# Moving stores behind their copies, and a strided bias load, in a fused scan, attention and experts kernel

## Chip, cores and metric

The kernel runs on one core of one Trainium2 chip, written in Bass with the Tile layer under a manual schedule. The metric is device time in microseconds (us), the median of three runs. All data are 32-bit floats.

## What is computed

Four images of 384 channels and 32x32 positions go through two layers. The reference, cut to what matters:

```python
# layer 0: four-direction selective scan, B=4, D=384, L=1024, N=16 states
x = x + _L0_conv_ref(_gn(x), ...)
#   per direction k: dt = softplus(W_dt (W_x x)); Bs, Cs = rows of W_x x
    def step(h, inp):
        dtt, ut, bt, ct = inp
        dA = jnp.exp(dtt[..., None] * A)
        h = h * dA + (dtt * ut)[..., None] * bt[:, :, None, :]
        y = jnp.einsum('bkdn,bkn->bkd', h, ct)
        return (h, y)
#   the four directions are summed, normalised over channels, gelu
# layer 1: attention over 1024 tokens (one head of 384, causal), then 4 experts, top 2
t = _to_tokens(x)
t = t + _L1_attn_ref(_ln_t(t), Wq, Wk, Wv)
t = t + _L1_ffn_ref(_ln_t(t), gate_w, gate_b, w1, b1, w2, b2)
#   ffn: h = gelu(x w1 + b1); y = h w2 + b2; out = sum of gate * y over the chosen two
x = _from_tokens(t, x)
```

## The kernel before, in words

The scan sets the clock of the whole program. It is cut into 768 units: 4 images (b), 3 blocks of 128 channels (m), 4 directions (k), 4 groups of 4 states (q), 4 groups of 32 channels (j). Each unit is a tile of 128 partitions (32 channels by 4 states) by 1024 positions. the main loop (from L2090 on) runs a counter `t`, the tick, and emits one unit's work in each: `decay` on ScalarE (ACT) makes `da` = exp(dt * a); `front` (L705) on VectorE (DVE) makes `v` = du * B; `middle` (L711) on DVE is the scan itself, h = h * da + v; `back` (L728) on GpSimd (POOL) multiplies h by C; `row` (L753) on TensorE (PE), every fourth tick, sums over the states into `y` in PSUM. For the first image, part of the `v` tiles are made on PE and ACT instead (`feed` and `turned`, L1017).

Beside the scan, `preparation(b)` makes the inputs of the next image: group norm, the projections, softplus, and in `project_dt` the product du = dt * u (L576). It stores dt and du in DRAM (L578, L579). `fetch` loads them back, repeated over the states: dt five ticks ahead of its use (L666, four buffers), du three ticks ahead (L666), and the B and C rows (`bc`, L677, two buffers, one pair of loads in four ticks) three ticks ahead. These loads, and nearly all others, are issued by SyncE (SP), which takes its instructions strictly in the order in which they were emitted.

Layer 1 of image b runs beside the scan of image b+1. `attention` makes the scores, the softmax and the values; `rows` (from L1236) takes each block of 128 tokens out of PSUM with an ACT copy into `yb` (L1240) and stores it to `t2_d` at once (L1242). `experts` runs 11 blocks of 256 tokens, each through two weight matrices, six weight tiles for each (L1627); `out_` copies a block's result to the tile `yt` on ACT (L1793), stores it to `ys_d` at once (L1795), and gives the tile's slot back. Later `combine` gathers these rows (L1832), reads `t2_d` again, and writes the output. The last image has no scan beside it: its attention and experts (`alone` in the code) form the tail of the kernel.

The work in a tick is ordered by hand. A generator yields `"wait", n` to go on n ticks later. `defer(n, f)` runs `f` at the start of tick t + n; with `inner` as third argument, in the middle of it. The tiles of layer 1, of the preparation and of the weights share eight `slots`: a generator that finds none free waits for the next tick, and a slot that is given may be taken a tick later. All this is decided when the program is built; on the chip only semaphores hold the engines to it.

`later` runs once, from tick 8 on: it loads small constants, one DMA a tick (L333), among them the bias b2 of the experts in three loads, each turned from expert-last to expert-first by its access pattern (4x128 single values); then it sums `d_skip` on DVE (L336), waits 40 ticks, zeroes a tile on POOL (L339), and stores it over the tables `xs_d` and `ys_d` in eight DMAs of 1.5 MB, six ticks apart (L343). In `within`, a flag is computed on DVE that chooses a cheaper softplus; one tick later (L514) POOL and ACT are told to load it (L515).

Of the kernel before, what the change touches and what calls it, by code (L numbers as in the profile page):

```python
# [17 lines left out]
P = 128  # L18
B = 4
C = 384  # L20
M = C // P
# [33 lines left out]
NBLK = 2 * L // BT + E - 1  # L55
# [3 lines left out]
def hybrid_kernel(  # L59
# [22 lines left out]
    nc = tc.nc  # L82
# [41 lines left out]
    def defer(ticks, f, where=due):  # L124
        where.setdefault(clock[0] + ticks, []).append(f)

    class Shared:
# [6 lines left out]
        def ready(self, n=1):  # L134
            return len(self.free) >= n and self.free[n - 1][0] <= clock[0]
# [69 lines left out]
    t2_d = [dram.tile([L, C], F32, tag=f"t2_{b}", name=f"t2d_{b}") for b in range(B)]  # L205
# [113 lines left out]
    b2s = const.tile([E, C], F32, tag="b2s", name="b2s")  # L319
# [6 lines left out]
    def later():  # L326
        yield "wait", 8
        for t, src in (
            (dsk, d_skip), (lnw, ln_w), (lnb, ln_b),
            (gw, gate_w.rearrange("(c p) e -> p c e", p=P)), (gb, gate_b.partition_broadcast(P)),  # L330
            *((b2s[:, m * P : (m + 1) * P], b2[:, :, m].rearrange("p e -> e p")) for m in range(M)),
        ):
            nc.sync.dma_start(t, src)  # L333
            yield "wait", 1
        yield "wait", 2
        nc.vector.tensor_reduce(dsum, dsk, AX.X, ALU.add)  # L336
        yield "wait", 40
        zero = yield from slots.take("zero", P, C)
        nc.gpsimd.memset(zero, 0.0)  # L339
        yield "wait", 2  # L340
        for t in (*xs_d, *ys_d):
            for o in range(0, E * CAP, 8 * P):
                nc.sync.dma_start(  # L343
                    t[o : o + 8 * P, :].rearrange("(r p) d -> p r d", p=P),
                    zero.unsqueeze(1).to_broadcast([P, 8, C]),
                )
                yield "wait", 6
        slots.give("zero")

# [148 lines left out]
    def within(b, xd):  # L500

        top = sm.tile([P, 1], F32, tag="top", name=f"top_{b}")
        nc.vector.tensor_reduce(top, xd, AX.X, ALU.max, apply_absolute_value=True)
        nc.vector.tensor_mul(top, top, steep)
        yield "wait", 1
        ps = yield from banks.take(f"top_{b}")
        nc.tensor.matmul(ps[:1, :K], top, mine_k, start=True, stop=True)
        yield "wait", 1
        most = sm.tile([1, 1], F32, tag="most", name=f"most_{b}")
        nc.vector.tensor_reduce(most, ps[:1, :K], AX.X, ALU.max)  # L510
        banks.give(f"top_{b}")
        fit = sm.tile([1, 1], I32, tag="fit", name=f"fit_{b}")
        nc.vector.tensor_tensor(fit, most, room, ALU.is_le)
        yield "wait", 1  # L514
        fits[b] = nc.values_load(  # L515
            fit, engines=[mybir.EngineType.Pool, mybir.EngineType.Activation],
            min_val=0, max_val=1,
        )
# [584 lines left out]
    def attention(b, yb, fx0):  # L1103

        alone = b == B - 1
# [17 lines left out]
        for h in range(NH):  # L1123
            for m in range(M):
                s = bass.ts(h, 512)
# [85 lines left out]
        def group_rows(q0, n):  # L1211

            if q0 + n > 4 and b not in routes:
                routes[b] = Route(b)
            return [
                fx0[:, q, :] if q < 4 else routes[b].rows[:, q - 4, :] for q in range(q0, q0 + n)
            ]
# [3 lines left out]
        def values(i):  # L1221
            name = f"po_{b}_{i}"
            po = yield from banks.take(name)
            s = bass.ts(i, P)
            for m in range(M):
                nc.tensor.matmul(
                    po[:, m * P : (m + 1) * P], yb[:, m, s], ident, start=(m == 0), stop=False
                )
            for j in range(i + 1):
                nc.tensor.matmul(  # L1230
                    po[:, :C], pts[i][:, j, :], vt[:, j, :], start=False, stop=(j == i)
                )
            yield "pe", 1.2 + 0.65 * (i + 1)
            slots.give(f"pt_{b}_{i}")

            def rows():  # L1236
                stat = sm.tile([P, 6], F32, tag="stat", name=f"stat_{b}_{i}")
                nc.vector.bn_stats(stat, po[:, :C])
                nc.vector.bn_aggr(moments[:, i, :], stat)
                nc.scalar.copy(yb[:, :, s], po[:, :C].rearrange("p (m t) -> p m t", m=M))  # L1240
                banks.give(name)
                nc.sync.dma_start(  # L1242
                    t2_d[b][s, :].rearrange("p (m t) -> p m t", m=M), yb[:, :, s]
                )
                for h, (q0, n) in enumerate(GROUPS):
                    if i == q0 + n - 1:
                        defer(1, lambda h=h, q0=q0, n=n: side.append(
                            ready(b, h, yb, group_rows(q0, n), moments)
                        ))

            defer(1, rows, inner)
# [334 lines left out]
    def experts(b, route):  # L1586

        alone = b == B - 1
# [42 lines left out]
        def need(key):  # L1631

            n = chunks.index(key)
            while fetched[0] <= n:
                while not slots.ready():
                    yield "wait", 1
                weights()
            while fetched[0] < min(n + 4, len(chunks)) and slots.ready(1 + slots.kept):
                weights()

        def rows_of(t, j):
            return t.rearrange("(k i p) d -> k p i d", p=P, i=BT // P)[bass.ds(block[j], 1)].rearrange(
                "o p i d -> p (o i) d"
            )
# [41 lines left out]
        def by_rows(j, run, fill):  # L1686

            if not alone:
                run(BT)
                return  # L1690
            with tc.If(filled[j] > P) as whole:
                run(BT)
            with whole.Else():
                fill(P)
                with tc.If(filled[j] > 0) as some:
                    run(P)
                with some.Else():
                    fill(0)
# [57 lines left out]
        def second_(j, gone):  # L1756
            pss = {}
            for c0 in range(0, 6, STEP):
                for c in range(c0, c0 + STEP):
                    yield from need(("2", j, c))  # L1760
                if c0 == 0:
                    for i in range(2):
                        pss[i] = yield from banks.take(f"py_{b}_{j}_{i}")
                    while clock[0] < gone:

                        yield "wait", 1

                def run(n):
                    for c in range(c0, c0 + STEP):
                        for f in range(2):  # L1770
                            for i in range(n // P):
                                nc.tensor.matmul(  # L1772
                                    pss[i][:, :C], hts[j][:, 2 * c + f, i * P : (i + 1) * P],
                                    tiles["2", j, c][0][:, f, :],
                                    start=(c == 0 and f == 0), stop=(c == 5 and f == 1),
                                )

                def fill(o):
                    if c0 == 0:
                        for m in range(M):  # L1780
                            nc.tensor.transpose(pss[o // P][:, bass.ts(m, P)], ident, ident)

                by_rows(j, run, fill)
                slots.give(*[tiles["2", j, c][1] for c in range(c0, c0 + STEP)])
                yield "pe", PART * STEP
            yt = yield from slots.take(f"yt_{b}_{j}", P, 2, C)

            def out_():
                for i in range(2):
                    if alone and i == 1 and j < NBLK - 1:  # L1790
                        nc.vector.tensor_copy(yt[:, i, :], pss[i][:, :C])  # L1791
                    else:
                        nc.scalar.copy(yt[:, i, :], pss[i][:, :C])  # L1793
                    banks.give(f"py_{b}_{j}_{i}")
                nc.sync.dma_start(rows_of(ys_d[0], j), yt)  # L1795
                slots.give(f"yt_{b}_{j}")
                if alone and j == 2:
                    side.append(beside_all(b))
                elif alone and j == NBLK - 2:
                    side.append(first_choice(b))  # L1800
                elif j == NBLK - 1:
                    side.append((late if alone else combine if b < B - 2 else held_back)(b))

            defer(1, out_, inner)
# [278 lines left out]
    assert clock[0] < -2  # L2083
    clock[0] = -2
    side.append(later())
    side.append(feed())
    decay(0)
    decay(1)
    t = 0
# [88 lines left out]
```

## Time and profile before

| | |
|---|---|
| median of three runs | 3706.41 us (3705.7 to 3707.15) |
| profiled execution, its own time | 3699.47 us |
| its span, first to last instruction | 3697.7 us, mean granted TensorE clock 0.869 |
| last scan of the last image begins | 3124.9 us |
| busy: PE, DVE, ACT, POOL | 2972.1, 2910.4, 2058.5, 1977.7 us |
| DMA moved | 798.44 MB, mean 216 GB/s |
| SyncE's issues: weights, bc, dt, du | 528, 384, 192, 192 |
| SyncE's issues: `t2d` (L1242), `ysd` from `yt` (L1795) | 32 of 192 KB, 44 of 384 KB |

How to read it. A group line of the profile gives line, engine, operation, tiles (out<-in) and count, then busy time and mean duration in ns, then the idle time of the engine just before these instructions and what ended it. A line of waits gives who waited for what: total us, times, longest. "SPq" is SyncE, which only issues and waits. The chain of work that ended last is followed back from the last instruction, with its shares by engine.

### The profile page before, as it was taken

What the parts mean: (1) busy time and instruction counts of PE and PEld (TensorE: products, weight loads), DVE (VectorE), ACT (ScalarE), POOL (GpSimd) and SP (SyncE); (2) the same over time, 40 slices, a digit from 0 to 9 for tenths busy, and PEclk for the clock granted to TensorE, in tenths of its full rate; (3) what the DMA queues carried; (4) which work ended last, traced back from release to release, by engine and by line L of the source; (5) the groups of instructions that cost most, each with busy time, mean ns of one, the idle gap of its engine ahead of it and who ended that gap; (6) DMA issues with size and microseconds to landing.
All of it is one profiled execution on the core that took longest, in us unless ns stands there. A gap on an engine that the chain in (4) does not pass through costs nothing.

```text
span 3697.7 us, 41309 instructions
## 1 busy us (share of the span) xinstructions
PE 2972.1 (80%) x13258; PEld 1779.7 (48%) x13258; DVE 2910.4 (79%) x2169; ACT 2058.5 (56%) x3256; POOL 1977.7 (53%) x939
## 2 busy tenths in 40 slices
PE   4565766778499999668679999769589999788998
PEld 1332433334166555334345656334256664566776
DVE  6898898989979899998989889999989998120000
ACT  4787888656466666456556666345456555242221
POOL 2676777645646556764655556765666666010001
PEclk7677777789599999879789999879789999889997
DMA  6666665445568888654477878563478876115655
GB/s 189 208 250 249 252 216 207 180 170 178 188 233 294 297 279 300 210 183 154 164 247 277 289 263 305 186 209 117 146 253 299 298 278 227 56 65 164 203 189 167
DMA packets 405203, 798.44 MB, mean 216 GB/s; under 512 B 47500, under 2 KB 278620, under 8 KB 404972
## 3 DMA queue, kind: packets, MB, share of 16 engines
q1 hardware_dynamic: 390572, 770.01, 59.7%
q0 software_dynamic: 8192, 25.17, 2.0%
q8 instruction: 118, 1.93, 0.2%
q10 hardware_dynamic: 6208, 0.39, 0.1%
q14 instruction: 113, 0.93, 0.1%
HBM read 680.44 MB, written 115.02 MB: 215 GB/s over the span
## 4 chain that ended last, share of the span: by engine, by line
DVE 40%; PE 39%; DMA 7%; ACT 7%; issue 5%; SPq 1%; POOL 1%; DVEq 0%; ACTq 0%; POOLq 0%
DVE h L711 22%; DVE v L705 13%; PE ph L1722 10%; PE py L1772 8%; PE y L753 4%; DMA w<-in_w 3%; ACT st L195 2%; DMA du<-dts 2%; ACT da L195 2%; PE pq L1129 2%; PE pdt L561 2%; PE v_end L1772 2%; PE pv L1140 1%; PE y_end L1772 1%; PE v L1017 1%
## 5 line engine op out<-in xcount | busy, mean ns | idle before, releaser
L728 POOL TENSOR_TENSOR h<-h,bc 128x1024 f32<-128x1024 f32 x768 | 1817.7, 2370 | 1180.3 <-DVE v L705 1022.3
L711 DVE TENSOR_TENSOR_SCAN h<-da,v 128x1024 f32<-128x1024 f32 x768 | 1749.0, 2283 | 62.3 <-PE v L1017 26.2
L195 ACT ACTIVATE da<-dt,a 128x1024 f32<-128x1024 f32 x768 | 882.2, 1158 | 728.0 <-DVE h L711 595.5
L705 DVE TENSOR_TENSOR v<-du,bc 128x1024 f32<-128x1024 f32 x664 | 867.7, 1307 | 152.0 <-PE y L753 58.4
L753 PE MATMUL y<-h,sel 128*32 128x512 f32 x3072 | 573.5, 696 | 199.6 <-POOL h L728 189.1
L1722 PE MATMUL ph<-turned,w 128*128 128x256 f32 (+1 forms) x2784 | 639.5, 387 | 57.3 <-DMA w<-in_w 44.9
L1722 PEld LDWEIGHTS ph<-turned,w 128*128 128x128 f32 x2784 | 529.7, 195 | 173.3 <-issue 49.0
L1772 PE MATMUL py<-w,ht 128*128 128x384 f32 x1704 | 576.6, 490 | 6.7 <-DMA w<-in_w 6.7
L1772 PEld LDWEIGHTS py<-w,ht 128*128 128x128 f32 x1704 | 319.0, 190 | 261.8 <-issue 39.6
L195 ACT ACTIVATE ht<-ph,b1t 128x256 f32<-128x256 f32 x470 | 196.9, 472 | 313.5 <-PE ph L1722 292.8
L753 PEld LDWEIGHTS y<-h,sel 128*32 128x32 f32 x3072 | 105.0, 119 | 535.1 <-POOL h L728 309.3
L1832 POOL DMA_INDIRECT g<-ysd,places x64 | 84.2, 1316 | 342.2 <-DMA ysd<-yt 326.5
L195 ACT ACTIVATE st<-turn,bt 128x128 f32<-128x128 f32 x832 | 242.9, 541 | 0.1
L1017 PE MATMUL v<-ident,st 128*128 128x128 f32 x832 | 151.7, 344 | 102.9 <-DVE h L711 98.5
L1017 PEld LDWEIGHTS v<-ident,st 128*128 128x128 f32 x832 | 124.4, 179 | 150.3 <-DVE h L711 84.1
L185 ACT ACT_TABLE_LOAD x120 | 154.0, 1283 | 12.9 <-issue 10.8
L561 PE MATMUL pdt<-xd,wdt 12*128 12x512 f32 x184 | 108.2, 737 | 29.1 <-ACT st L195 13.7
L1482 POOL DMA_INDIRECT xsd<-fx,places x32 | 38.1, 1191 | 135.7 <-issue 133.9
L1791 DVE COPY yt<-y_end 128x384 f32<-128x384 f32 x3 | 1.7, 559 | 130.9 <-ACT ht L195 63.3
L1230 PE MATMUL po<-vt,pt 128*128 128x384 f32 x234 | 89.6, 533 | 11.5 <-ACT pt L1120 11.5
L195 ACT ACTIVATE ht<-ht 128x3072 f32<-128x3072 f32 x33 | 91.3, 2766 | 0.4
L1159 PE MATMUL ss<-axn,qt 128*128 128x512 f32 (+3 forms) x240 | 87.4, 506 | 2.4 <-ACT pt L1120 1.3
(417 smaller groups left out, 2593.5 us busy)
## 6 DMA issues: line engine op xcount, KB each, us to landing
w<-in_w SPq DMA_DIRECT2D x528, 384.0 KB
bc<-rows SPq DMA_DIRECT2D x384, 512.0 KB
dt<-dts SPq DMA_DIRECT2D x192, 512.0 KB
du<-dts SPq DMA_DIRECT2D x192, 512.0 KB
dts<-dt SPq DMA_DIRECT2D x48, 512.0 KB
dts<-du SPq DMA_DIRECT2D x48, 512.0 KB
xg<-xsd SPq DMA_DIRECT2D x44, 384.0 KB
ysd<-yt SPq DMA_DIRECT2D x44, 384.0 KB
```

What stands on the lines that cost most here:

```text
L185: nc.scalar.preload_act_table_set(kind)
L195: return nc.scalar.activation(dst, src, f, **more)
L561: nc.tensor.matmul(pss[i], wdt[r, m * P : (m + 1) * P], xd[r, bass.ts(h, 512)], start=True, stop=True,)
L705: return nc.vector.tensor_tensor(u["v"], spread["du4", n], spread["bc", n][:, 0, :], ALU.mult)
L711: nc.vector.tensor_tensor_scan(u["h"][:, ::step], u["da"][:, ::step], u["v"][:, ::step], 0.0, op0=ALU.mult, op1=ALU.add,)
L728: product = units[n]["product"] = nc.gpsimd.tensor_tensor(h, h, spread["bc", n][:, 1, :], ALU.mult)
L753: units[n]["row"] = nc.tensor.matmul(y, sel, h, start=first, stop=last, tile_position=(0, jj * DJ))
L1017: nc.tensor.transpose(u["v"][:, t * P : (t + 1) * P], st[:, t, u["j"] * P : (u["j"] + 1) * P], ident)
L1159: nc.tensor.matmul(ps[:, : e - o], qt[:, c, i * P : (i + 1) * P], xn[o // 512][:, c, : e - o], start=(c == 0), stop=(c == M - 1 and (alone ...
L1230: nc.tensor.matmul(po[:, :C], pts[i][:, j, :], vt[:, j, :], start=False, stop=(j == i))
L1722: nc.tensor.matmul(ps[:, i * BT : i * BT + n], t[:, c, i * P : (i + 1) * P], xt[:, c, :n], start=(c == 0), stop=(c == M - 1),)
L1772: nc.tensor.matmul(pss[i][:, :C], hts[j][:, 2 * c + f, i * P : (i + 1) * P], tiles["2", j, c][0][:, f, :], start=(c == 0 and f == 0), stop ...
```

## The change

Three things are changed. The three loads of b2 go from the middle of `later` to its end, after the last zero store, four ticks apart; what stood after them in `later` comes three ticks earlier. The stores L1242 and L1795 are put into a function `kept`, which is run two ticks after the copy, except for the last image, and, for the experts, except for the last of the 11 blocks; the slot of `yt` is given in the same function. In `within`, the flag is loaded two ticks after it is computed for all images but the first.

```diff
@@ later
-            *((b2s[:, m * P : (m + 1) * P], b2[:, :, m].rearrange("p e -> e p")) for m in range(M)),
...
         slots.give("zero")
+        for m in range(M):
+            nc.sync.dma_start(b2s[:, m * P : (m + 1) * P], b2[:, :, m].rearrange("p e -> e p"))
+            yield "wait", 4
@@ within
-        yield "wait", 1
+        yield "wait", 1 if b == 0 else 2
@@ attention, rows()
-                nc.sync.dma_start(
-                    t2_d[b][s, :].rearrange("p (m t) -> p m t", m=M), yb[:, :, s]
-                )
+
+                def kept():
+                    nc.sync.dma_start(
+                        t2_d[b][s, :].rearrange("p (m t) -> p m t", m=M), yb[:, :, s]
+                    )
+
+                if alone:
+                    kept()
+                else:
+                    defer(2, kept)
@@ experts, out_()
+                if alone or j == NBLK - 1:
+                    kept()
+                else:
+                    defer(2, kept)
+
+            def kept():
                 nc.sync.dma_start(rows_of(ys_d[0], j), yt)
                 slots.give(f"yt_{b}_{j}")
                 if alone and j == 2:
```

The lines after these in `out_` (what is started after the third, the tenth and the last block) move into `kept` with them.

## The prediction

> **What bounds the kernel now.** First view: the page, its chain and its groups.
>
> ```profile
> DVE 40%; PE 39%; DMA 7%; ACT 7%; issue 5%; SPq 1%; POOL 1%; DVEq 0%; ACTq 0%; POOLq 0%
> L711 DVE TENSOR_TENSOR_SCAN h<-da,v 128x1024 f32<-128x1024 f32 x768 | 1749.0, 2283 | 62.3 <-PE v L1017 26.2
> L705 DVE TENSOR_TENSOR v<-du,bc 128x1024 f32<-128x1024 f32 x664 | 867.7, 1307 | 152.0 <-PE y L753 58.4
> ```
>
> VectorE (DVE) carries the scan to about 3127 us: 768 ticks, each one product (1.31 us) and one scan (2.28 us), at least 3.63 us with the small gaps between. Then the last image's attention and experts follow, where TensorE (PE) is busy. Whatever shortens the scan shortens the kernel, if nothing else takes over.
>
> Second view: the three stages in which an image's experts run beside the next image's scan (start:end, then busy time of PE, PEld, DVE, ACT, POOL, granted clock, DMA share, GB/s).
>
> ```profile
> 1081.00:1465.00 384.00, 372.27 (x1588) 231.88 (x1588) 355.28 (x205) 250.03 (x310) 226.89 (x96) 0.99 0.83 291
> 1904.00:2238.00 334.00, 313.76 (x1336) 198.71 (x1335) 295.33 (x170) 215.98 (x267) 188.91 (x81) 0.96 0.80 281
> 2714.00:3070.00 356.00, 349.61 (x1572) 228.86 (x1571) 343.18 (x193) 221.69 (x280) 226.44 (x96) 1.00 0.80 283
> ```
>
> PE is idle for 12, 20 and 6 us, DVE for 29, 39 and 13: they are nearly equal bounds, and DMA is 80% busy. The 96, 80 and 96 ticks at 3.63 us, with the next image's products (L576, 1.53 us each, some ten, eight and none), need 364, 303 and 349 us. So 20 + 31 + 7 = 58 us is all that any help in these stages can give.
>
> Third view: SyncE's own waits. It issues nearly every DMA in the order of the program, so each wait holds up all behind it.
>
> ```profile
> SPq L677 <- POOL h L728: 666.0, 118, 22.0
> SPq L1242 <- ACT yb L1240: 268.9, 28, 54.6
> SPq L1795 <- ACT yt L1793: 233.9, 38, 15.9
> ```
>
> L677 is the pace of two buffers, which stays. The other two are stores waiting for the copy just emitted. In the three expert stages L1795 waits 57.4 + 60.3 + 49.7 us, in the three attention stages L1242 waits 61.5 + 70.4 + 60.4 us.
>
> Fourth view: whom this hurts. DVE's waits between 1081 and 1465, then between 838 and 930 (attention of the first image):
>
> ```profile
> DVE v L705 <- DMA du<-dts: 13.2, 7, 3.1
> DVE v L705 <- DMA bc<-rows: 4.6, 2, 2.9
> DVE v L705 <- PE y L753: 4.4, 2, 3.9
> ```
> ```profile
> DVE nb L1176 <- PE ss L1164: 1.7, 1, 1.7
> DVE stat L1238 <- PE po L1230: 1.0, 2, 0.9
> DVE v L705 <- DMA du<-dts: 0.6, 1, 0.6
> ```
>
> So the attention stores hold SyncE up for 61.5 us and cost DVE at most 0.6; the loads are far enough ahead. The expert stores do cost. Fifth view, the timeline of DVE:
>
> ```profile
> 1142.17 2.29 DVE L711 TENSOR_TENSOR_SCAN h<-da,v 128x1024 f32<-128x1024 f32 x1
> 1147.52 1.23 DVE L705 TENSOR_TENSOR v<-du,bc 128x1024 f32<-128x1024 f32 x1 [3.06 <-DMA du<-dts]
> ```
>
> SyncE had sat at L1795 for 6.1 us until 1140.15; the du load behind it was issued at 1141.27 and DVE went on at 1147.52.
>
> Sixth view, SyncE's timeline at the start, where the bias b2 is loaded:
>
> ```profile
> 103.31 0.49 SPq L333 DMA_DIRECT2D b2s<-in_b  x1
> 103.91 5.42 SPq L666 DMA_DIRECT2D dt<-dts  x1
> ...
> 111.13 0.86 SPq L333 DMA_DIRECT2D b2s<-in_b  x1
> 112.04 4.93 SPq L666 DMA_DIRECT2D du<-dts  x1
> ...
> 118.12 1.47 SPq L333 DMA_DIRECT2D b2s<-in_b  x1
> 119.64 3.19 SPq L666 DMA_DIRECT2D du<-dts  x1
> ```
>
> An issue of such a load takes 0.55 us otherwise; behind each b2 load it takes 5.42, 4.93 and 3.19. DVE's waits between 98 and 135 us hold `du<-dts` with 8.7 us in three, at 116.2, 122.4 and 128.2, each just after one of these.
>
> **What the Trainium skill says.** "DMA: Bandwidth & Descriptors", section Anatomy of one DMA: DMA engines do not wait on semaphores; the wait is in the issuing sequencer. The trace agrees: 6.1 us at L1795 before the du load. The same page, Rules for kernel authors: an access whose last dimension is not contiguous becomes one descriptor per element. A b2 load reads 4x128 values across its source, and the trace holds 510 to 533 packets of 4 bytes in the two us after 108, 116 and 122. "Perfetto Trace Analysis", section DMA Instruction — HWDGE: the recorded issue lasts until its descriptors are made. That fits the 3 to 5 us, though no run yet shows that the b2 load alone causes them.
>
> **The change, part by part.**
>
> *Bias loads.* Removed from ticks 13 to 15: the three waits, 8.7 us, in a stretch where PE is idle for half the time and DVE sets the pace. Added at ticks 105, 109 and 113 (about 420 to 450 us): the excess issue, 4.9 + 4.4 + 2.6 = 12 us of SyncE. What hides it: they are 4 ticks apart, dt is loaded 5 ticks ahead and du 3, and DVE there waits for `v` from PE (444.65, 3.41 us), that is, those units do not use du at once. Without that cover it costs the 8.7 us again. I take 7 gained, bounds 0 and 9.
>
> *Zero tables.* The eight 1.5 MB stores and the reduction of dsum come 3 ticks earlier, so they pass other loads on SyncE. Today du and bc are late by 6.8 + 3.7 us between 300 and 460 us, around these stores. In the new order the fourth stands ahead of the burst of dt loads instead of inside the du loads, the second just ahead of a du load. I take 0, bounds -8 and +5.
>
> *Attention stores* (24, images 0 to 2, two ticks later). SyncE waits less, DVE had nothing to gain: 0, bounds -3 and +1. The last image's stores stay, and so does the 54.6 us wait.
>
> *Expert stores* (10 of 11 in each of images 0 to 2; the eleventh stays). Each DVE wait for du, bc or turned rows that follows within some 15 us of a wait at L1795: 3.06, 2.86, 1.54, 1.71, 2.06 in the first stage; 3.85, 1.08, 1.06, 2.73, 0.90 in the second; 1.41, 1.07 in the third. Sum 23.3. PE's waits for weights in the same places (4.81, 3.52, 0.93; 0.78, 1.39, 0.80; 1.77, 1.88, 0.71, 0.77) are 17.4, and mostly lie beside them. Two ticks are 7.3 us against 6 us of mean wait, so most of the wait goes. But what is late next: the loads still follow L677's and L666's waits, PE is nearly full, and the DMA engines are 80% busy. I take two thirds of 23.3, 15 gained; bounds 5 and 29 (with the 2.03 and 3.92 that DVE waits for `y` after such weights).
>
> *What the two ticks cost.* The slot of yt is held two ticks longer. By the built order of instructions the weights keep their lead of 2 to 3 ticks, experts shift by at most one or two ticks, and image 2's experts and the tail keep their order. But the preparation of images 2 and 3 takes slots later: its products come 1 to 5, then 5 to 6 ticks later (last ones at 383 and 535 instead of 378 and 530), and their four 0.5 MB stores meet other loads. Weight loads wait 54.5 us for the slot of such a store today (L1627 <- DMA dts<-dt); about 14 us of DVE waits follow those. I take 0, bounds -8 and +8, since positions only shuffle. The extra tick ahead of the loaded flag (L514) takes at most 1 us from ACT and POOL, neither the bound: 0.
>
> *Sum*: 7 + 0 + 0 + 15 + 0 = 22 us. The profiled execution took 3699.47 us (span 3697.7); 3677 after. The median of the runs, 3706.41, is 7 us (0.19%) above that execution; the same 22 us off gives 3684.
>
> **Rivals.**
>
> 1. *Hidden anyway.* Both engines are at their bound in the expert stages; DVE's waits are slack against PE, and earlier loads only wait in their buffers. For it: PE idle only 12 us of 384. Against: DVE idles longer than PE in all three, and the third stage runs at 3.7 us a tick once no such waits occur. Only the bias gain less a shuffle remains: -4, 3702.
>
> 2. *A larger gain.* SyncE is late as a whole, and 58 us of excess are its doing; with 167 us of waits gone two thirds of that go, 38 us, and the bias 7: -45, 3661. Against: some 24 us of the excess follow waits for PE or for the preparation's stores.
>
> 3. *Slower: the preparation's stores meet the weights.* Place: L1627 behind L578/L579 in images 1 and 2. Price: one such meeting today left PE idle for 8.35 us (2177 us), with 5 us of DVE waits behind it. It must eat the 22 us and 7.4 more, 29 us: from four further such meetings among the twenty-four later products (4 x 8.35 = 33 us) the kernel is slower, +11, 3718. Against: equal work at other ticks is as likely to part as to meet.
>
> 4. *It doesn't do what it says*: the store still waits after two ticks. Mean wait 6 us, longest 10 in these stages, against 7.3: it would only leave tails, and is in the first rival.
>
> **How the numbers follow.** Forecast (10 to 35 us gained) 0.55; larger gain 0.18; hidden 0.18; slower 0.09. A measurement of this kernel can tell about 0.2%, 7.4 us, from no change; forecast and larger gain lie beyond it: faster 0.73, same 0.18, slower 0.09. Range: upward it reaches over the hidden case to 3708, downward to 3660, which takes in most of the larger gain; it leaves out about 0.09 below and 0.1 above.
>
> **What would show it.** In the changed profile, L1795 <- ACT yt falls from 167 us in the three stages to under 50; DVE's waits for du and bc in the stages of the first two fall from 27 us to under 14; no 8.7 us at 98 to 135 us, and the three long issues appear at 420 to 455 with no DVE wait over 1 us behind. Attention stages stay as long as they are within 3 us each. Wrong, if DVE waits for `PE y` grow by what du's shrink (rival 1), or weights wait longer for dts stores (rival 3).

## The result, and the profile after

The changed kernel takes 3660.73 us (median of four runs, 3659.31 to 3665.99) where the kernel before takes 3706.45 (3705.7 to 3707.15): ratio 0.9879, 95% interval [0.9862, 0.9896]. That is 45.7 us off, twice the 22 us forecast. The profiled execution took 3660.66 us, its span 3659.0, its granted clock 0.868.

First the page's groups, in the order of those of before. Every line below the edit has moved: 711 is now 713, 705 is 707, 753 is 755, 1242 is 1246, 1795 is 1810, 1627 is 1636, 333 is 349.

```profile
L713 DVE TENSOR_TENSOR_SCAN h<-da,v 128x1024 f32<-128x1024 f32 x768 | 1749.2, 2283 | 66.7 <-PE v L1019 29.4
L707 DVE TENSOR_TENSOR v<-du,bc 128x1024 f32<-128x1024 f32 x664 | 862.0, 1298 | 90.0 <-PE y L755 46.5
```

The scan and the product cost what they did (2283 ns as before, 1298 after 1307). What fell is the idle time ahead of the product, from 152.0 to 90.0 us.

Next the busy table of the three stages with experts and scan, cut at the same ticks as before (start:end, length, busy time of PE, PEld, DVE, ACT, POOL, granted clock, DMA share, GB/s).

```profile
1072.00:1447.00 375.00, 368.94 (x1581) 230.24 (x1580) 354.77 (x203) 247.47 (x309) 226.60 (x96) 0.99 0.84 294
1881.00:2197.00 316.00, 308.51 (x1339) 192.77 (x1339) 296.12 (x171) 214.33 (x268) 189.25 (x81) 1.00 0.84 298
2671.00:3023.00 352.00, 349.87 (x1575) 229.41 (x1575) 343.93 (x194) 222.27 (x282) 226.72 (x97) 1.00 0.82 286
```

They were 384, 334 and 356 us long, 58 us in all over what their ticks need; now they are 375, 316 and 352, 27 over. So 31 us came from here. PE's idle time fell from 12, 20 and 6 us to 6, 7 and 2, with nearly the same busy time (3 and 5 us less in the first two).

SyncE's own waits, over the whole run, and then at the expert stores in each of the three stages:

```profile
SPq L679 <- POOL h L730: 783.0, 142, 21.7
SPq L1246 <- ACT yb L1242: 117.1, 22, 54.6
SPq L1810 <- ACT yt L1802: 69.8, 22, 8.3
```
```profile
SPq L1810 <- ACT yt L1802: 11.6, 4, 3.9
```
```profile
SPq L1810 <- ACT yt L1802: 7.3, 2, 3.7
```
```profile
SPq L1810 <- ACT yt L1802: 10.8, 6, 3.6
```

The expert stores held SyncE for 167 us in these stages and now do for 30; the attention stores for 192 us, now 12.4, 11.9 and 16.2. The 54.6 us wait of the last image stays, as its store was not moved. SyncE now spends more of its time at L679, waiting for one of the two `bc` buffers (783.0 us, 666.0 before). This is what one expects when SyncE has caught up and only the buffers hold it back.

DVE's waits for `du` and `bc` before, in the second of these stages (the first is shown in the prediction):

```profile
DVE v L705 <- DMA du<-dts: 6.6, 3, 2.7
DVE v L705 <- DMA bc<-rows: 3.0, 3, 1.1
```

After, DVE's waits in the first of these stages, then PE's waits for weights in the second:

```profile
DVE dt L578 <- ACT du L195: 8.2, 2, 7.4
DVE v L707 <- PE y L755: 3.4, 4, 1.9
DVE v L707 <- DMA du<-dts: 2.2, 2, 1.2
```
```profile
PE ph L1731 <- DMA w<-in_w: 2.8, 2, 1.8
PE py L1781 <- DMA w<-in_w: 2.5, 2, 1.7
```

`du` and `bc` together cost DVE 27.4 us in the first two stages before and 4.0 after. PE's waits for weights in the second stage fell from 12.6 us (11.8 for the first weight matrix, `ph`, and 0.8 for the second, `py`) to 5.3. One wait is new: 7.4 us of DVE in the first stage, for the softplus on ACT (`du`), ahead of one product of the next image; e5 shows where it comes from.

Where the scan got shorter can be read from the starts of its 768 units. In microseconds against the profiled execution of before, by stretch of ticks; "experts 1" is the stretch beside the experts of the first image, and so on:

| kernel | 16-31 (old bias place) | 272-367 (experts 1) | 400-415 | 464-559 (experts 2) | 656-767 (experts 3) | whole scan |
|---|---|---|---|---|---|---|
| changed kernel | -6.3 | -8.3 | -7.7 | -18.7 | -5.0 | -47.7 |
| e1, bias alone | -7.3 | -0.1 | -0.7 | -2.9 | -0.9 | -11.0 |
| e2, attention stores alone | -0.2 | -1.1 | +0.5 | -0.6 | -0.2 | +0.1 |
| e3, expert stores alone | -2.9 | -10.4 | -0.4 | -12.2 | -4.6 | -30.8 |
| e4, slot held alone | -2.9 | +1.1 | +0.5 | -4.4 | -1.0 | -5.9 |
| e5, flag alone | -2.2 | +2.1 | -7.9 | -6.9 | -0.1 | -10.9 |
| e6, zero tables alone | -1.1 | +0.8 | -0.3 | -0.7 | -0.2 | -1.7 |
| e7, all but the flag | -6.8 | -9.7 | -0.7 | -13.6 | -4.9 | -41.4 |

Read it with a spread in mind: among kernels in which nothing that bears on a stretch was changed, 16-31 varies from -0.2 to -3.1 and experts 2 from -0.6 to -2.9. Nothing in the prediction spoke of the stretch 400-415.

The changed kernel's tail, after its last scan has begun, is 582 us long in its profiled execution and 573 in that of before. That is not the change: it is 574 to 576 us in e1 to e8, 581 to 582 in e9 to e12, which ran on another chip and of which one (e11) has only the expert stores moved. The kernel before itself had medians of 3699 to 3701 us beside the first group and 3708 beside the second, and 3706 beside the changed kernel. So each ratio below is to the kernel before on the same chip, and what a change gives in us is (1 - ratio) times the median of that kernel; the bracket is the 95% interval of the ratio.

### The profile page after: what moved, and what is told of

It reads as the page before. It is cut to its first block, busy times and chain, and to the rows that moved or that the text cites. A ratio compares the mean times of both kernels' runs of the same rounds, so it can differ in the third digit from the quotient of the medians.

```text
span 3659.0 us, 41310 instructions
## 1 busy us (share of the span) xinstructions
PE 2970.2 (81%) x13258; PEld 1776.6 (49%) x13258; DVE 2907.3 (79%) x2169; ACT 2058.0 (56%) x3258; POOL 1977.6 (54%) x939
## 5 line engine op out<-in xcount | busy, mean ns | idle before, releaser
L713 DVE TENSOR_TENSOR_SCAN h<-da,v 128x1024 f32<-128x1024 f32 x768 | 1749.2, 2283 | 66.7 <-PE v L1019 29.4
L707 DVE TENSOR_TENSOR v<-du,bc 128x1024 f32<-128x1024 f32 x664 | 862.0, 1298 | 90.0 <-PE y L755 46.5
L1731 PE MATMUL ph<-turned,w 128*128 128x256 f32 (+1 forms) x2784 | 631.5, 383 | 35.3 <-DMA w<-in_w 29.1
L1847 POOL DMA_INDIRECT g<-ysd,places x64 | 83.6, 1307 | 345.3 <-DMA ysd<-yt 329.5
L185 ACT ACT_TABLE_LOAD x122 | 156.5, 1283 | 13.0 <-issue 10.9
```

The source lines that it names most:

```text
L185: nc.scalar.preload_act_table_set(kind)
L707: return nc.vector.tensor_tensor(u["v"], spread["du4", n], spread["bc", n][:, 0, :], ALU.mult)
L713: nc.vector.tensor_tensor_scan(u["h"][:, ::step], u["da"][:, ::step], u["v"][:, ::step], 0.0, op0=ALU.mult, op1=ALU.add,)
L1731: nc.tensor.matmul(ps[:, i * BT : i * BT + n], t[:, c, i * P : (i + 1) * P], xt[:, c, :n], start=(c == 0), stop=(c == M - 1),)
```

## Experiments

The theory was that SyncE's order is the whole mechanism: the bias loads and the expert stores each give what they held up, and attention stores, zero tables, the held slot and the flag give nothing. The rival was that part of the 45 us comes from somewhere else, the drift of the preparation or the timing of the slots.

### e1: the bias alone

The zero tables keep their ticks.

```diff
-            *((b2s[:, m * P : (m + 1) * P], b2[:, :, m].rearrange("p e -> e p")) for m in range(M)),
...
-        yield "wait", 2
+        yield "wait", 5
...
         slots.give("zero")
+        for m in range(M):
+            nc.sync.dma_start(b2s[:, m * P : (m + 1) * P], b2[:, :, m].rearrange("p e -> e p"))
+            yield "wait", 4
```

> Only the three bias loads are moved; the zero tables keep their ticks. Theory (SyncE is held up by the 4-byte pieces of each bias load, and the du loads behind it come late): the 8.7 us that VectorE waits between 98 and 135 us go, nothing comes back at 430 to 460 us, so 6 to 8 us are gained, 3699 to 3700. Rival (the early gain of the whole change came from the shifted zero tables or from chance): within 2 us of before.

Measured: 0.9972 [0.9961, 0.9984], 10.4 us off (3690.80 against 3700.52). DVE's waits at 96 to 135 us, where `du` alone had 8.7:

```profile
DVE v L707 <- DMA bc<-rows: 2.2, 1, 2.2
DVE v L707 <- DMA du<-dts: 1.6, 2, 1.4
```

The wait for `du` fell to 1.6; the wait for `bc` was 2.5 and stays. But the profiled execution of before happened to be slow at this place. In the stretch 16-31 the seven other kernels that leave the bias alone wait 5.7 to 8.1 us for `du`, the six with moved bias loads 1.0 to 2.2; the seven average -2.2 us against before, the six -7.0 (-6.3, -7.3, -6.8, and -6.0, -7.8, -7.8 for e9, e10 and e12). So the traces give the move 4.8 us. The time's interval, 6 to 14 us, agrees with the 7 of the prediction and hardly with 5; another few us of e1's 11 in the scan are spread over stretches in which nothing was edited, and stay unexplained.

At the new place, SyncE's issues in the changed kernel, then in e1 (start, then the time from the start of the first issue to the end of the last in that line):

```profile
417.46 0.48 SPq L349 DMA_DIRECT2D b2s<-in_b  x1
418.04 5.31 SPq L668 DMA_DIRECT2D dt<-dts  x1
...
435.00 0.53 SPq L349 DMA_DIRECT2D b2s<-in_b  x1
```
```profile
410.04 0.50 SPq L349 DMA_DIRECT2D b2s<-in_b  x1
412.58 0.51 SPq L668 DMA_DIRECT2D dt<-dts  x1
...
431.15 0.33 SPq L349 DMA_DIRECT2D b2s<-in_b  x1
431.58 2.51 SPq L679 DMA_DIRECT2D bc<-rows  x2
```

The slow issue follows the b2 load to its new place. In the changed kernel only one of the three loads has another DMA at once behind it, and that one takes 5.31 us. Where 2.0 us or more lie between, the next issue takes its ordinary 0.5. In e1 two of the three have a pair of `bc` loads at once behind them, and the first of the pair takes 1.86 and 1.66 us, where 0.59 is ordinary; so the price depends on what follows. Each such issue ends while the 4-byte packets of the b2 load run (the 5.31 us end at 423.36, most of the packets run from 422.3 to 423.8), so it is this load that holds it up. But a slow issue is not peculiar to 4-byte loads: in before, the first `du` load behind a zero store takes 4.33 us, at 325.12. DVE has no wait for a DMA in all of 396 to 460 us in the changed kernel.

### e2: the attention stores alone

```diff
+                if alone:
+                    kept()
+                else:
+                    defer(2, kept)
```

(`kept` holds the store of `t2_d`.)

> Only the attention stores come two ticks later. Theory (prefetched loads cover these waits): SyncE's wait at them falls from 192 us to under 60 in the three attention stages, and the time stays within 3 us of before. Rival (every microsecond of SyncE counts): 10 us or more gained.

Measured: 0.9994 [0.9981, 1.0006], 2.2 us off, which is no difference that can be told. SyncE's wait at the store falls from 192 us to 57 in the three stages (in the whole run from 268.9 to 133.2, of which 54.7 is the last image's). 136 us less waiting on an engine, and no time.

### e3: the expert stores alone

```diff
+                if alone or j == NBLK - 1:
+                    kept()
+                else:
+                    defer(2, kept)
+
+            def kept():
                 nc.sync.dma_start(rows_of(ys_d[0], j), yt)
                 slots.give(f"yt_{b}_{j}")
```

> Only the expert stores, with the slot of yt, come two ticks later. Theory (held-up loads): this alone brings most of the 46 us, 30 to 40 us gained, 3667 to 3677, and VectorE's waits for du and bc in the first two expert stages fall from 27 us to under 10. Rival (the gain is spread over the parts and their shifts): under 20 us gained.

Measured: 0.9934 [0.9916, 0.9951], 24.4 us off, interval 18 to 31. That is the largest part of the whole, but less than the 30 to 40 that the theory named. The store's wait in the three stages is 9.7 + 7.8 + 10.5 = 28 us (167 before). DVE's waits in experts 1, then in experts 2:

```profile
DVE v L705 <- PE y L753: 4.8, 2, 4.6
DVE v L705 <- DMA du<-dts: 3.5, 3, 2.4
DVE dt L576 <- ACT du L195: 1.6, 2, 1.0
DVE v L705 <- DMA bc<-rows: 0.9, 2, 0.7
```
```profile
DVE v L705 <- PE y L753: 11.5, 2, 9.3
DVE dt L576 <- DMA bc<-rows: 4.1, 1, 4.1
DVE v L705 <- DMA du<-dts: 2.8, 3, 2.0
```

The products' waits for `du` and `bc` are 4.4 and 2.8 us. Waits for `PE y` are 16.3 together, 13.4 before: little took the place of what went. The three stretches are 27 us shorter.

### e4: the store at once, the slot held two ticks longer

This parts the delay of the store from the longer hold.

```diff
                 nc.sync.dma_start(rows_of(ys_d[0], j), yt)
+                if alone or j == NBLK - 1:
+                    kept()
+                else:
+                    defer(2, kept)
+
+            def kept():
                 slots.give(f"yt_{b}_{j}")
```

> The expert store stays where it was, at once behind its copy, but the slot of yt is given two ticks later, so that the preparation of images 2 and 3 moves by the same ticks as in the changed kernel. Theory (the wait at the store is what costs): within 5 us of before, and L1795 still waits about 167 us. Rival (the gain comes from the later slots, which part the preparation's stores from the weight loads and move the group norm of the image after next): 10 us or more gained.

Measured: 0.9992 [0.9984, 1.0001], 3 us off, interval -0.4 to 6: no difference that can be told. SyncE and DVE in experts 1:

```profile
SPq L1795 <- ACT yt L1793: 57.8, 9, 8.2
```
```profile
DVE v L705 <- DMA du<-dts: 10.6, 7, 3.0
DVE v L705 <- PE y L753: 6.5, 3, 3.8
DVE v L705 <- DMA bc<-rows: 6.5, 3, 2.7
```

57.8 us at the store, as before (57.4), and 17.1 us of DVE waits for `du` and `bc` (17.8 before). So the hold alone is worth 6 us at most, and the gain of e3 is mainly the store's place on SyncE. One premise of this experiment did not hold: the longer hold does not move the preparation as the changed kernel does. The products of image 2 stay at their ticks and only the last few of image 3 come later, as in e3. The drift itself is tried in e5.

### e5: the flag alone

```diff
-        yield "wait", 1
+        yield "wait", 1 if b == 0 else 2
```

> Only the flag of the softplus is loaded two ticks behind its making, for all images but the first. By the built order this alone moves the preparation of image 2 by 1 to 5 ticks and that of image 3 by 5 to 6, with the group norm of image 3 from tick 408 to 413. Theory A (the flag is the missing part: the projections of image 3 no longer crowd TensorE at ticks 400 to 415, where VectorE waited 8.9 us for y): 7 to 15 us gained. Theory B (positions only shuffle, as predicted): within 4 us of before.

Measured: 0.9980 [0.9970, 0.9990], 7.4 us off, interval 4 to 11: theory A, at its lower end. The prediction had put it at nothing. The order of the instructions says what it moves: the flag's wait stands in the preparation, and everything after it in the preparation of images 2 and 3 follows. With this edit alone the products of L576 come at exactly the ticks they have in the changed kernel (last ones at 383 and 535 for images 2 and 3). With the stores moved and the flag left (e3), those of image 2 stay where they were (last at 378) and only the last few of image 3 shift, to 532. So the drift that the prediction put down to the held slot comes from the flag, but for the last few products of image 3.

A part of what it gains is seen in the stretch 400-415. There, in before, six projection matmuls of the next image (L469) stood between the matmuls of the attention, twice, ahead of the row sum `y` on PE. PE's timeline of before, then DVE's wait there:

```profile
1657.32 2.74 PE L469 MATMUL pxd<-x,wx 128*128 128x512 f32 x6
...
1664.40 2.74 PE L469 MATMUL pxd<-x,wx 128*128 128x512 f32 x6
...
1670.94 1.92 PE L753 MATMUL y<-h,sel 128*32 128x512 f32 x16
```
```profile
DVE v L705 <- PE y L753: 8.9, 1, 8.9
```

And the changed kernel in the same stretch, PE and then DVE:

```profile
1647.00 1.92 PE L755 MATMUL y<-h,sel 128*32 128x512 f32 x16
...
1658.63 1.88 PE L471 MATMUL pxd<-x,wx 128*128 128x512 f32 x4
```
```profile
DVE gn_rstd L447 <- ACT gn_rstd L195: 5.1, 1, 5.1
```

The group norm of image 3 now reaches its `gn_rstd` at tick 413 instead of 408, so its projections come after the row sum; the 8.9 us wait is gone. The two groups of six take 5.5 us of PE; what made up the rest of the 8.9 was not tried. In its place the group norm, which waited for nothing at tick 408, waits 5.1 us for ACT. e5 shows the same: no wait for `y`, and 4.7 us for `gn_rstd`. Over all kernels the stretch is -7.5 to -7.9 with the flag's extra tick (changed kernel, e5, e9, e12) and -0.7 to +0.5 without it (nine kernels).

That stretch flatters the flag. In the four ticks ahead of it, 396 to 399, the same four kernels are 4.5 us longer and the nine others unchanged: some of DVE's other work (two `yb` and a reciprocal) has moved from the one stretch into the other. Over ticks 368 to 463 together the kernels with the flag's tick are 4.3 to 4.7 us shorter than before (without e12, which was edited there), about the 8.9 that went less the 5.1 that came; the nine others lie between -2.9 and +2.7. The flag also costs something: in the four kernels with it, the product at tick 321 waits 6.4 to 7.4 us for the softplus on ACT, and in none of the others does any product wait for ACT more than 2 us in that stage. As a whole that stage still comes out near what it is without the flag (e5 2.1 us longer than before, e9 1.8 shorter than e10).

### e6: the zero tables alone

```diff
-        yield "wait", 40
+        yield "wait", 37
```

> Only the zero tables come three ticks earlier (a wait of 37 instead of 40); the bias loads stay. Theory: within 4 us of before, VectorE's waits for du and bc between 300 and 460 us move but do not vanish. Rival: 5 us or more gained, since the fourth store no longer stands among the du loads.

Measured: 1.0002 [0.9994, 1.0010]. Nothing, as forecast.

### e7: the changed kernel without the flag's extra tick

```diff
-        yield "wait", 1 if b == 0 else 2
+        yield "wait", 1
```

> The changed kernel with the flag loaded after one tick as before; stores and bias as changed. Theory A (flag worth 7 to 15 us): 7 to 15 us slower than the changed kernel, 3668 to 3676. Theory B (flag worth nothing): 3659 to 3664.

Measured: 0.9898 [0.9883, 0.9913], 37.7 us off. In the table it has all of the changed kernel's gains but the 7 us in 400-415, of which 4.5 are moved work, and 5 of those in 464-559. Its time, 3659.98, is what theory B named, but the kernel before is 7 us faster here (3699.26) than beside the changed kernel, and the intervals of the two ratios overlap: this run alone does not decide.

### e9 and e10: the changed kernel again, with and without the flag's tick

e7 and the changed kernel were not measured side by side. These two were, on one chip; e10 is e7's code.

> The changed kernel once more, on the same chip as the next three. If the parts add up (bias 10, expert stores 24, flag 7, the rest nothing) it is 41 us, 1.1%, faster than before; if part of the 46 us was a difference between chips, it is 30 to 38.

> The changed kernel with the flag loaded after one tick, on the same chip as the changed kernel. Theory A (flag worth 7 us, as alone): 5 to 12 us slower than the changed kernel beside it. Theory B (the flag gains only while the stores hold SyncE up): within 3 us of it.

Measured: 0.9879 [0.9864, 0.9894] with, 0.9902 [0.9887, 0.9918] without; medians 3663.11 and 3670.25, 7.1 us apart. The flag is worth inside the changed kernel what it is worth alone, as theory A said. With the flag the gain is 44.9 us, interval 39 to 50: as much as in the first measurement, so no part of it need be put down to chips.

### e8 and e11: expert stores one tick and four ticks later

e3's edit with `defer(1, kept)` and `defer(4, kept)`.

> Only the expert stores, one tick later instead of two. Theory (the store waits until the copy is done, 6 us in the mean, and one tick is 3.6 us): SyncE still waits 70 to 130 us at them in the three stages, and 10 to 18 us are gained instead of 24. Rival (it is enough that a few loads pass the store): the same 24 us as with two ticks.

> Only the expert stores, four ticks later. Theory (after two ticks little is left to wait for): 22 to 30 us gained, as with two ticks, and under 30 us of SyncE's waits are left at the stores in the three stages. Rival (a slot held longer starves the weights): less gained than with two ticks.

Measured: one tick 0.9941 [0.9927, 0.9954], 21.8 us off; four ticks 0.9908 [0.9895, 0.9922], 34 us off; two ticks were 24.4. SyncE's wait at the store in experts 1, with one tick:

```profile
SPq L1801 <- ACT yt L1793: 29.1, 9, 6.2
```

With 18.3 and 28.7 in the other two it is 76 us of the 167; with two ticks 28; with four no such line is left in any. So half the wait gone brings most of the gain, and the waits short of 4 us that two ticks leave cost little. The theory's 10 to 18 us for one tick was too low: 21.8, with an interval of 17 to 27, cannot be told from two ticks, as the rival said, though SyncE's wait was as the theory said. In the traces the three expert stretches add up to -22.6 us with one tick, -27.2 with two and -26.6 with four: between two and four nothing is seen, though the times, on two chips, differ by 10 us (34 us with an interval of 29 to 39, 24.4 with 18 to 31). Whether four beat two is left open.

### e12: the next image's first weights ahead of a gather that waits

If the gain comes from SyncE's order, changing that order should pay in another place too. At the start of the experts, SyncE issues the gather of the first tokens (L1660), which waits for the scatter that makes them, and the first weights stand behind it. Changed kernel between 970 and 1030 us: SyncE, PE, DVE.

```profile
SPq L1660 <- DMA xsd<-rows,places: 13.4, 3, 7.8
```
```profile
PE ph L1731 <- DMA w<-in_w: 10.1, 1, 10.1
```
```profile
DVE v L707 <- PE y L755: 9.3, 1, 9.3
```

One chain: a gather waits 7.8 us for its rows; the weights behind it are late; PE waits 10.1 us for them; `y` behind that product on PE is late, and the scan waits 9.3 us. The edit, on top of the changed kernel, asks for three weight tiles first:

```diff
+        while fetched[0] < 3:
+            while not slots.ready():
+                yield "wait", 1
+            weights()
         yield from load(0)
```

> The changed kernel, and the first three weight tiles of an image's experts are fetched ahead of the load of its first block, which waits for the scattered rows. Theory (SyncE's order is the lever: what stands behind a waiting DMA comes late, here TensorE waits about 10 us for weights at the start of the stage and VectorE 9 us for y after it): 8 to 20 us faster than the changed kernel. Rival (TensorE is full there, and the work only moves): within 4 us of it.

Measured: 0.9805 [0.9792, 0.9818], 3634.41 us, 72 us below the kernel before and 28.7 below the changed kernel on the same chip (3663.11). It is more than either forecast. DVE's waits and PE's, between 970 and 1025 us, are now

```profile
DVE v L707 <- ACT da L195: 0.8, 1, 0.8
```
```profile
PE y L755 <- POOL h L730: 9.7, 2, 5.6
PE pxg L1669 <- DMA xg<-xsd: 4.5, 1, 4.5
PE gn_var L395 <- DVE gn_g_var L392: 2.9, 1, 2.9
```

with no wait for weights, though the gather still waits (11.4 us). At the other two starts PE's waits for weights (4.6 and 7.3 us in e9) are gone as well, and PE's wait for the gathered rows stays. The three starts of the experts, ticks 256-271, 448-463 and 640-655, are 10.5, 5.7 and 5.6 us shorter (the first and third against before, the second against the changed kernel, which had 3.1 more than before there): 22 of the 28.7.

## Why the prediction was right or wrong, step by step

The mechanism and the sign were right, the size was half. The time lies at the lower edge of the range, which was drawn so wide to take in most of rival 2; that it holds is owed to this width, not to the sum. The parts measured alone add up: 0.0028 (bias) + 0.0066 (expert stores) + 0.0020 (flag) + 0.0006 (attention) - 0.0002 (zero tables) = 0.0118, against 0.0121 for the whole. Within the intervals, nothing that can be told is owed to the parts meeting.

*Bias loads, 7 us.* Right in kind: the 8.7 us went (1.7 us of `du` waits left), and the cover at the new place held. Of the three long issues forecast there, 12 us, one of 5.31 us appeared, since nothing stood at once behind the other two loads. By time 10.4 us, interval 6 to 14, 7 inside it; by the traces about 5. The prediction took the 3 to 5 us for the making of the load's own descriptors. The trace puts it otherwise: the b2 load's own issue takes 0.48 us at 417.46, and it is the issue behind it that lasts until the 4-byte packets run.

*Zero tables, 0; attention stores, 0.* Both right (e6 1.0002, e2 0.9994). The attention stages kept their length within some 3 us where only the stores were moved. In the changed kernel the second of them (ticks 408 to 449) is the exception, 194 us long instead of 201, and that is the flag (194 us in e5 too, 200 in e7), in part because two products of the next image now come after it.

*Expert stores, 15 us.* Mis-sized: 24.4 (18 to 31). The list of DVE waits, 23.3 us, agrees with the measurement; 15, after a third was taken off for "what is late next", lies outside its interval. The waits for `y` grew by only 3 us (13.4 to 16.3 us in the first two stages), the weights came earlier too (PE waited 22.7 us for them in these stages before, 12.7 in e3), and the drop of the three stretches, 27 us, is near the prediction's bound of 29 (of the two waits that this bound adds, the one of 2.03 us, at 1284.4, is in the trace a wait for `du`, not for `y`). That PE is nearly full was no ground for the discount: PE had been waiting at the same places, and its waits shrank with DVE's.

*What the two ticks cost, drift 0.* Right for the slot: e4 shows nothing that can be told for the hold. Wrong in its cause, since nearly all of the drift is the flag's. Wrong in "positions only shuffle" too: the drift was worth 7 us, which only the bounds of 8 either way took in. The feared meetings did not come: weights waiting for the slot of a `dts` store (L1636) went from 54.5 us to 35.7.

*The flag, "at most 1 us from ACT and POOL, neither the bound: 0".* This is the step that failed outright: 7.4 us in e5, 7.1 between e9 and e10. It priced the two engines that load the flag and not what is queued behind the wait in the generator, all the preparation of an image. The 8.9 us wait for `y` and the projections ahead of it stand in the trace of before; only its sign and size after a shift of five ticks could not be read there.

*Rival 1, hidden anyway*: excluded by e3, in which the three expert stretches got 27 us shorter. *Rival 3, slower*: it did not happen. *Rival 2, a larger gain*: its number (3661) is the measured one, but not its account. It took 38 us from the 58 in the expert stages. 31 went there, some 5 of these by the flag (-18.7 against -13.6 in 464-559), and a few more came from the flag in the attention stage. The total is right partly by luck. *Rival 4*: no, the stores wait 30 us instead of 167.

Of the signs named: L1795 under 50 us (30), `du` and `bc` under 14 (4.0), no 8.7 at 98 to 135 and no new DVE wait at 420 to 455 all came. Three long issues at 420 to 455 did not, and the second attention stage did not keep its length.

Still open: why the flag is worth 5 to 7 us in 464-559, where e4, which only holds the slot, shows 4.4, and how its gains and its new wait at tick 321 come to 7 in all; the several us of e1 outside the edited stretch.

## What to carry to other kernels

On an engine that issues DMAs in order, look for each instruction that waits for something just made (a store behind its copy, a gather behind its scatter), and ask what independent load stands behind it and which engine runs dry; only those that end in another engine's wait are worth moving, whatever their own total (here 136 us less of waits gave nothing, 139 us less gave 24). Where each wait can be named and nothing else is late in the trace at the same moment, do not discount them without a reason: here the list came out in full. When a one-tick edit stands in a generator, count everything that the generator emits afterwards, and compare what then stands ahead of the bound's input on every engine.

## What the runs showed of the hardware

- The load of b2 in pieces of 4 bytes (4x128 values) is issued in 0.33 to 1.47 us, and a DMA issued on SyncE at once behind it (0.04 to 0.11 us) pays: a `dt` or `du` load takes 3.2 to 6.9 us over all traces, 0.52 in the median elsewhere, and a `bc` load 1.7 and 1.9 us in e1, 0.59 elsewhere. It takes its ordinary 0.5 when 2.0 us or more lie between the end of the one issue and the start of the next.
- The same tail of the program, with the same instructions and PE busy for 501 to 504 us in each, took 574 to 576 us in eight runs on two chips and 581 to 582 in four runs on a third. The granted clocks, 0.886 to 0.890 and 0.884 to 0.885, hardly differ; what makes the 7 us is not shown. So times of two kernels that ran on different chips can differ by this much with no change to the program.
